# An attention block with a mixture of experts: the first part ordered anew, places' experts found on partitions, and own memory for each third first matrix

## The chip, the cores and the metric

The kernel runs on one core of a Trainium2 chip. The metric is the device time of one execution in microseconds (us); it is given as the median of three runs. The engines are TensorE (PE; its weight loads are listed as PEld), VectorE (DVE), ScalarE (ACT), GpSimd (POOL) and SyncE (SP), which here only issues transfers. Each engine works through its own list in order and waits on semaphores of the others.

## The reference

The input x has 2 sequences of 2048 tokens with 256 channels. It is normalized once, and the result goes into two branches whose outputs are added to x.

```python
xn = layernorm(x)
# branch 1: time mixing
h = layernorm(xn) * ln_g + ln_b
last = shift h by one token (zero at the start of a sequence)
k = (h * mix_k + last * (1 - mix_k)) @ Wk.T      # v and r alike
num, den = scans over the tokens: num = num * td + exp(k) * v ; den = den * td + exp(k)
a = sigmoid(r) * (num / (den + 1e-8)) @ Wo.T
# branch 2: a mixture of 8 experts, 2 for each token
s = relu(xn @ Wr + br); the best two of 8, softmax over them
f = sum over the two of weight * (relu(xn @ W1[e] + b1[e]) @ W2[e] + b2[e])
out = x + a + f
```

## The kernel before, in words

The 4096 tokens are cut into 8 blocks of 512 tokens, four per sequence; a block is held as four rows of 128 tokens on the partitions. The kernel has two parts.

The first part does, for each block: `stats` (mean and variance of its four rows with bn_stats and bn_aggr on VectorE, L190 and L191, then a power of -0.5 on POOL, L200), `normed` (both normalizations at once: x2 = (x - mean) * rr for each row, three rows on VectorE, L224, and one on ScalarE, L226; then a write of x2 to a table in HBM), `turned` (eight transposes on TensorE, L244, copied by ScalarE into x2T for the router and, with ln_g and ln_b, into xaT for the time mixing, L247 and L248; xaT has one more column in front, the last token of the block before, which POOL writes, L237 or L239), `scored` (router products, L262), and `routed` (the scores turned back, L273).

Then there are the mixes. Each block needs three blends of now and last (k, v, r), numbered 0k, 0v, 0r, 1k and so on to 7r. `mix(n)` makes the next n of the 24 blends: for blocks 0 to 2 VectorE forms dx = now - last (L301) and then two operations L310 for each blend; for blocks 3 to 7 ScalarE first makes last * (1 - mix) (L285, two steps for each blend, which `pieces` issues one after each of its own steps once NFIRST steps are done), and VectorE adds the rest (L310). `some(n)` makes the next n of the 48 pieces: one output half of a projection, two matrix products on TensorE (L339, four records in the profile) and one ScalarE eviction into kvr (L342). Blend i serves pieces 2i and 2i + 1.

When all eight blocks are routed, `best_two` on VectorE finds each token's two experts (L371 to L394); two products with a triangle and with ones (`pre`, L559) give each token's rank; a long list of small VectorE operations (L572 to L655) turns ranks into places. A loop of eight groups over `inv` (L736 to L755) then builds one-hot tables on VectorE and multiplies them on TensorE, which gives the token of each place: `into` and `frm`. `experts_of_places` finds which expert each place belongs to (`whose`, `whose_i`): a place is a pair of units of 128 tokens or a single unit, and the expert is the number of limits that lie at or below the place's number. It does so with all 39 places along the free axis, the same in each partition. `experts_later` fills `mine` (L722), a mask by place and expert.

The second part is a loop over 37 steps, one for each place. Each gathers its tokens' rows from the table (POOL, L874), loads one expert's matrices (`load_first`: b1 and w1, L857 and L859; `load_second`: b2 and w2, L865 and L867; all issued on SP, with the expert's number read from whose_i), and does two products (hp at L914, yp at L927). The scans, gates and output products of the time mixing are spread over its first steps.

The order is fixed by hand: under `tc.manual_schedule()` each engine executes in the order in which the program text issues. The calls of stats, normed, mix, some and so on from L408 to L1003 are therefore the schedule, and `keep_warm(n)` puts n matrix products without use (L405) into TensorE's list. Memory is taken from pools; a pool opened after another is closed can lie on the memory of the closed one, and its first writers then wait for the last users of that. wpool, with the experts' matrices, is opened after the routing pool is closed and waits in this way. A pool's `bufs` gives how many buffers of one tag rotate: w1 and b1 have three, mixes six, x2 three, the tables of the inv loop three.

Of the kernel before, what the change touches and what calls it, by code (L numbers as in the profile page):

```python
# [9 lines left out]
F32 = mybir.dt.float32  # L10
# [4 lines left out]
ALU = mybir.AluOpType  # L15
# [11 lines left out]
def rwkv_moe_block(  # L27
# [47 lines left out]
    KMAX = (NU + 1) // 2  # L75
# [14 lines left out]
    small = ctx.enter_context(tc.tile_pool(name="small", bufs=2))  # L90
    kvr_pool = ctx.enter_context(tc.tile_pool(name="kvr", bufs=NB // 2))
# [67 lines left out]
    nc.vector.memset(power, -0.5)  # L159
    prio = rout.tile([P, NT, E], F32, name="prio")  # L160
# [24 lines left out]
    def stats(b, i0=0, i1=NS):  # L185
        if i0 == 0:
            mvs[b] = (mk(f"st_{b}", [P, NS, 6]), mk(f"mv_{b}", [P, NS, 2]))
        st, mv = mvs[b]
        for i in range(i0, i1):
            nc.vector.bn_stats(st[:, i, :], xts[b][:, i, :])  # L190
            nc.vector.bn_aggr(mv[:, i, :], st[:, i, :])  # L191
        if i1 < NS:
            return
        mean, var = mv[:, :, 0], mv[:, :, 1]

        at = ts(b, NS)
        w = mk(f"w_{b}", [P, NS])
        nc.gpsimd.tensor_scalar(w, var, 1.0 + LN_EPS, LN_EPS * LN_EPS, ALU.mult, ALU.add)
        rrs[b] = rr_all[:, at]
        nc.gpsimd.tensor_tensor(rrs[b], w, power[:, 0:NS], ALU.pow)  # L200
        nc.gpsimd.tensor_scalar(ve_all[:, at], var, LN_EPS, 0.0, ALU.add, ALU.add)
        mrrs[b] = (mean, mk(f"mrr_{b}", [P, NS]))
# [12 lines left out]

    def normed(b):
        xt = xts[b]
        mean, mrr = mrrs[b]
        nc.vector.scalar_tensor_tensor(mrr, mean, -1.0, rrs[b], ALU.mult, ALU.mult)
        x2 = x2s[b] = rpool.tile([P, NS, C], F32, tag="x2", bufs=3, name=f"x2_{b}")  # L220
        for t in range(NS):
            r, m = rrs[b][:, t : t + 1], mrr[:, t : t + 1]
            if t:
                nc.vector.tensor_scalar(x2[:, t, :], xt[:, t, :], r, m, ALU.mult, ALU.add)  # L224
            else:
                nc.scalar.activation(x2[:, t, :], xt[:, t, :], AF.Identity, bias=m, scale=r)  # L226
        nc.sync.dma_start(table_t[:, ts(b, NS), 0:C], x2)

    x2Ts = [None] * NB

    def turned(b):
        x2 = x2s[b]
        x2T = x2Ts[b] = rpool.tile([P, NC, TB], F32, tag="x2T", name=f"x2T_{b}")

        xaT = xaTs[b] = xa_pool.tile([P, NC, TB + 1], F32, name=f"xaT_{b}")
        if b % BPS == 0:
            nc.gpsimd.memset(xaT[:, :, 0:1], 0.0)  # L237
        else:
            nc.gpsimd.tensor_copy(xaT[:, :, 0:1], xaTs[b - 1][:, :, TB : TB + 1])  # L239
        tps = []  # L240
        for c in range(NC):
            tp = ps_t.tile([P, TB], F32, tag="pt", name=f"tp_{b}_{c}")
            for t in range(NS):
                nc.tensor.transpose(tp[:, ts(t, P)], x2[:, t, ts(c, P)], ident)  # L244
            tps.append(tp)
            if b:
                nc.scalar.copy(x2T[:, c, :], tp)  # L247
            nc.scalar.activation(  # L248
                xaT[:, c, 1 : TB + 1], tp, AF.Identity, bias=vec(5, c), scale=vec(4, c)
            )  # L250
        if b == 0:
            for c in range(NC):
                nc.scalar.copy(x2T[:, c, :], tps[c])
# [40 lines left out]
    def blender():  # L294
        for b in range(NB):
            now, last = xaTs[b][:, :, 1 : TB + 1], xaTs[b][:, :, 0:TB]
            if b < NDX:

                dx = mixes.tile([P, NC, TB], F32, tag="dx", bufs=1, name=f"dx_{b}")
                for c in (slice(0, 1), slice(1, NC)) if b == 0 else (slice(0, NC),):  # L300
                    nc.vector.tensor_tensor(dx[:, c, :], now[:, c, :], last[:, c, :], ALU.subtract)  # L301
            for i in range(3):
                if b < NDX:
                    m = mixes.tile([P, NC, TB], F32, tag="mix", name=f"mix{i}_{b}")
                    by, other = dx, last
                else:
                    m = ahead.pop(0)
                    by, other = now, m
                for c in range(NC):
                    nc.vector.scalar_tensor_tensor(  # L310
                        m[:, c, :], by[:, c, :], vec(1 + i, c), other[:, c, :],
                        ALU.mult, ALU.add,
                    )
                blends[b].append(m)
                yield
# [9 lines left out]
    NFIRST = 12  # L325
# [80 lines left out]

    keep_warm(13)
# [51 lines left out]
    k_iota = count("k_iota", KMAX)  # L459
    u_iota = count("u_iota", NSING, base=2 * NPAIR)  # L460
# [23 lines left out]
    keep_warm(8)  # L484
    some(2)
    turned(1)
    nc.scalar.activation(td, cols[:, E * NH : E * NH + NC], AF.Exp)
    mix(2)
    some(2)
    scored(0)  # L490
    stats(2)
    stats(3)
    normed(2)
# [4 lines left out]
    mix(1)  # L498
    some(1)
    routed(1)  # L500
    normed(3)
    mix(1)
    some(1)
    turned(3)
    scored(2)
    some(1)
    stats(4)
    mix(1)
# [3 lines left out]
    turned(4)  # L512
    scored(3)
    stats(5)
    stats(6)
    divisors(0)
# [3 lines left out]
    turned(5)  # L520
    some(1)
    scored(4)
    stats(7)
    normed(6)
    some(1)
    routed(4)
    turned(6)
    scored(5)
    normed(7)
    divisors(1)  # L530
    mix(1)
    some(1)
    routed(5)
    turned(7)
    scored(6)
# [4 lines left out]
    mix(1)  # L540
# [27 lines left out]
    mix(3)  # L568
# [56 lines left out]
    mix(1)  # L625
    some(2)
    pos = rt("pos", (P, E, NT))
# [30 lines left out]
    some(2)  # L658
# [6 lines left out]
    def holds(nm, places, limits):  # L665

        n, k = places.shape[1], limits.shape[1]
        c = rt(f"{nm}_c", (P, n, k))
        nc.vector.tensor_tensor(
            c, places.unsqueeze(2).to_broadcast([P, n, k]),  # L670
            limits.unsqueeze(1).to_broadcast([P, n, k]), ALU.is_ge,
        )
        r = rt(f"{nm}_r", (P, n))
        nc.vector.tensor_reduce(r, c, AX.X, ALU.add)
        return r

    whose = rt("whose", (P, NW))

    def experts_of_places():
        limits = rt("limits", (P, 3, E))  # L680
        nc.vector.tensor_copy(limits[:, 0, :], fcum[:, 0, :])
        nc.vector.tensor_scalar(limits[:, 1, :], fcum[:, 1, :], full, None, ALU.add)
        nc.vector.tensor_scalar(limits[:, 2, :], fcum[:, 2, :], pairs, None, ALU.add)
        by_pair = holds("by_pair", k_iota, limits.rearrange("p a e -> p (a e)"))
        nth = rt("nth", (P, NSING))
        taken = rt("taken", (P, 1))
        nc.vector.tensor_scalar(taken, pairs, float(NPAIR), pairs, ALU.max, ALU.add)
        nc.vector.tensor_scalar(nth, u_iota, taken, None, ALU.subtract)
        by_single = holds("by_single", nth, fcum[:, 2, :])

        for i, n in enumerate((full, pairs)):
            after = rt(f"after{i}", (P, KMAX))
            nc.vector.tensor_scalar(after, k_iota, n, float(-E), ALU.is_ge, ALU.mult)
            nc.vector.tensor_tensor(by_pair, by_pair, after, ALU.add)
        nc.vector.tensor_copy(whose[:, 0:NPAIR], by_pair[:, 0:NPAIR])

        split = rt("split", (P, NSING))
        nc.vector.tensor_scalar(split, nth, 0.0, None, ALU.is_lt)
        n = KMAX - NPAIR
        part = rt("part", (P, 2 * n))  # L700
        nc.vector.tensor_copy(
            part.rearrange("p (a b) -> p a b", b=2),
            by_pair[:, NPAIR:KMAX].unsqueeze(2).to_broadcast([P, n, 2]),
        )
        part = part[:, 0:NSING]
        nc.vector.tensor_tensor(part, part, by_single, ALU.subtract)
        nc.vector.tensor_tensor(part, part, split, ALU.mult)
        nc.vector.tensor_tensor(whose[:, NPAIR:NW], part, by_single, ALU.add)
        nc.vector.tensor_scalar_min(whose, whose, float(E - 1))
        nc.vector.tensor_copy(whose_i, whose)  # L710
# [19 lines left out]
    MIX, SOME = (0, 1, 0, 1, 0, 1, 0, 1), (1, 1, 1, 2, 1, 1, 1, 0)  # L730
# [37 lines left out]
    nc.vector.tensor_scalar_min(frm, into, float(NTOK - 1))  # L768
    experts_of_places()
    mix(2)  # L770
    some(2)
# [82 lines left out]
    def load_first(s):  # L854
        ev = expert_of(s)
        b1_sb = wpool.tile([P, NH], F32, tag="b1", bufs=3, name=f"b1_{s}")
        nc.sync.dma_start(b1_sb, b1cols[bass.ds(ev, 1)].rearrange("a p h -> p (a h)"))  # L857
        w1_sb = wpool.tile([P, NC, H], F32, tag="w1", bufs=3, name=f"w1_{s}")
        nc.sync.dma_start(w1_sb, w1[bass.ds(ev, 1)].rearrange("a (c p) h -> p (a c) h", p=P))  # L859
        weights[s, 1] = (w1_sb, b1_sb)  # L860
# [89 lines left out]
    some(4)  # L950
# [115 lines left out]
```

## Time and profile before

| what | value |
|---|---|
| median of three runs | 665.88 us (664.79 to 666.34) |
| the profiled execution's own time | 665.95 us |
| its span | 664.3 us |
| mean granted TensorE clock | 0.99 |
| TensorE busy | 638.8 us, 96% |
| VectorE busy | 338.0 us, 51% |
| ScalarE busy | 230.4 us, 35% |
| POOL busy | 233.1 us, 35% |
| first hp product | 126.12 us from the start of the span |
| VectorE busy from 57.30 to 101.25 | 41.17 us of 43.95 |

How to read it: the span is the time from the first to the last recorded instruction, and the execution's own time has 1.65 us around it. Busy times are averages over the whole span, so an engine with a low share can still hold up another in one stage; that is read from the timeline and from the waits. An entry `a <- b` reads "a is made from b", and a bracket at the end of a row gives the idle time of the engine ahead of it and who ended it. The clock is the share of full speed that TensorE was granted.

### The profile page before, as it was taken

Reading aid. Unit: us, or ns where it says so; the run is one execution under the profiler, and the core shown is the slowest. Engines: PE = TensorE matmul, PEld = TensorE weight load, DVE = VectorE, ACT = ScalarE, POOL = GpSimd, SP = SyncE. Lnnn points to the kernel's source line nnn. Section 1 sums busy time; section 2 is a strip of 40 time slices with the busy share of each in tenths; the row PEclk is TensorE's granted clock in tenths of the full one; section 3 lists DMA queues with packets and bytes.
Section 4 is the critical chain, followed back from the end, with each engine's and each line's share of the span. In section 5 each row is a group of like instructions: output and inputs, shape, how many; then the busy total and the mean of one; then the engine's idle time right before and its main releaser. Section 6 shows DMA issues by size and latency. Waiting matters only on the chain. (4 is left out here: it accounts for less than half of the span.)

```text
span 664.3 us, 9082 instructions
## 1 busy us (share of the span) xinstructions
PE 638.8 (96%) x3038; PEld 498.2 (75%) x3038; DVE 338.0 (51%) x777; ACT 230.4 (35%) x474; POOL 233.1 (35%) x207
## 2 busy tenths in 40 slices
PE   7989997999999999999999999999999999999993
PEld 3544443688888888888888888888888888888882
DVE  7987996456356458576666667422222121222110
ACT  3776753423423323333333333222223222223320
POOL 5460204033343335313443434643434433334111
PEclk9999997999999999999999999999999999999998
DMA  8529101767976986699868686976566777666621
GB/s 279 167 96 299 19 1 50 238 210 215 308 186 196 298 202 196 178 341 254 225 166 227 170 223 142 269 185 205 168 176 182 215 213 220 168 176 182 200 34 17
DMA packets 92409, 124.50 MB, mean 187 GB/s; under 512 B 15452, under 2 KB 80552, under 8 KB 92232
## 3 DMA queue, kind: packets, MB, share of 16 engines
q1 hardware_dynamic: 74368, 100.99, 46.7%
q0 software_dynamic: 17472, 22.86, 18.6%
q8 instruction: 25, 0.41, 0.2%
q14 instruction: 24, 0.20, 0.1%
q10 hardware_dynamic: 520, 0.05, 0.1%
HBM read 105.89 MB, written 26.38 MB: 199 GB/s over the span
## 5 line engine op out<-in xcount | busy, mean ns | idle before, releaser
L918 ACT ACTIVATE h<-hp,b 128x256 f32<-128x256 f32 (+1 forms) x296 | 135.8, 459 | 348.5 <-PE hp L914 237.5
L914 PE MATMUL hp<-xT,w 128*128 128x256 f32 (+1 forms) x1184 | 251.8, 369 | 1.1 <-ACT h L918 0.4
L927 PE MATMUL yp<-w,h 128*128 128x256 f32 x1104 | 244.4, 379 | 0.0
L914 PEld LDWEIGHTS hp<-xT,w 128*128 128x128 f32 x1184 | 198.8, 189 | 49.5 <-ACT h L918 16.1
L927 PEld LDWEIGHTS yp<-w,h 128*128 128x128 f32 x1104 | 207.0, 190 | 26.6
L939 POOL DMA_INDIRECT out_dram<-y,into x50 | 82.4, 1648 | 213.5 <-DVE y L935 98.6
L904 DVE COPY xT<-xp 128x512 f32<-128x512 f32 (+1 forms) x37 | 24.3, 655 | 168.5 <-PE xp L902 163.3
L874 POOL DMA_INDIRECT xg<-table,frm x69 | 75.2, 1090 | 45.1 <-PE p L339 24.3
L934 DVE TENSOR_TENSOR y<-yp,b 128x256 f32<-128x256 f32 x67 | 28.3, 423 | 105.1 <-PE yp L927 105.1
L939 POOL DMA_INDIRECT acc<-y,into x19 | 31.9, 1679 | 92.9 <-issue 34.7
L813 DVE RECIPROCAL dn<-dn 128x512 f32<-128x512 f32 x16 | 53.6, 3353 | 0.5
L342 ACT ACTIVATE kvr<-p 128x512 f32<-128x512 f32 x48 | 28.7, 599 | 41.4 <-PE p L339 40.8
L339 PE MATMUL p<-mix,wr 128*128 128x512 f32 x64 | 32.7, 650 | 4.5 <-DVE mix L310 4.1
L339 PE MATMUL p<-mix,wk 128*128 128x512 f32 x64 | 30.1, 603 | 3.9 <-DVE mix L310 2.4
L339 PE MATMUL p<-mix,wv 128*128 128x512 f32 x64 | 29.6, 599 | 0.0
L822 PE MATMUL op<-wo,z 128*128 128x256 f32 x128 | 28.9, 379 | 0.0
L339 PEld LDWEIGHTS p<-mix,wr 128*128 128x128 f32 x64 | 12.7, 207 | 19.5 <-issue 17.0
L822 PEld LDWEIGHTS op<-wo,z 128*128 128x128 f32 x128 | 24.3, 190 | 3.3
L935 DVE TENSOR_SCALAR y<-y,gate 128x256 f32<-128x256 f32 x67 | 24.6, 367 | 2.4
L310 DVE SCALAR_TENSOR_TENSOR mix<-xaT,cols,mix 128x512 f32<-128x512 f32 x30 | 22.0, 779 | 7.0 <-ACT mix L285 6.9
L339 PEld LDWEIGHTS p<-mix,wk 128*128 128x128 f32 x64 | 11.5, 190 | 16.6 <-issue 12.2
L884 DVE TENSOR_SCALAR xg<-xg 128x256 f32<-128x256 f32 x69 | 22.1, 359 | 0.0
(176 smaller groups left out, 402.6 us busy)
## 6 DMA issues: line engine op xcount, KB each, us to landing
w<-in_L_ffn_W_dram SPq DMA_DIRECT2D x74, 1024.0 KB
b<-in_L_ffn_b_dram SPq DMA_DIRECT2D x37, 128.0 KB
table<-x SPq DMA_DIRECT2D x8, 512.0 KB
x<-in_L_attn_x_dram SPq DMA_DIRECT2D x7, 512.0 KB
out_dram<-o_sb POOLq DMA_DIRECT2D x5, 512.0 KB
acc<-o_sb POOLq DMA_DIRECT2D x3, 512.0 KB
xg<-table,frm POOLq DMA_INDIRECT x69
out_dram<-y,into POOLq DMA_INDIRECT x50
```

The source lines that it names most:

```text
L339: nc.tensor.matmul(p, w[:, c, ts(o, P)], m[:, c, :], start=(c == 0), stop=(c == NC - 1))
L342: nc.scalar.activation(kvr[b][:, i, o, :], p, f, scale=sign)
L813: nc.vector.reciprocal(dn, dn)
L822: nc.tensor.matmul(op, z[:, c, ts(t, P)], wo_sb[:, c, :], start=(c == 0), stop=(c == NC - 1))
L874: nc.gpsimd.indirect_dma_start(out=g, out_offset=None, in_=table, in_offset=bass.IndirectOffsetOnAxis(ap=frm[:, u : u + 1], axis=0), bound ...
L904: nc.vector.tensor_copy(xT, xp)
L914: nc.tensor.matmul(hp, w1_sb[:, c, ts(j, P)], xT[:, c, :], start=(c == 0), stop=(c == NC - 1))
L918: nc.scalar.activation(h[:, 0:n], hp, AF.Relu, bias=b1_sb[:, j : j + 1])
L927: nc.tensor.matmul(yp, hs[j][:, ts(i, P)], w2_sb[:, j, :], start=(j == 0), stop=(j == NH - 1))
L934: nc.vector.tensor_tensor(y, yp, b2_sb, ALU.add)
L935: nc.vector.tensor_scalar(y, y, gates[s][i], None, ALU.mult)
L939: return nc.gpsimd.indirect_dma_start(out=to, out_offset=bass.IndirectOffsetOnAxis(ap=into[:, u : u + 1], axis=0), in_=y, in_offset=None, ...
```

## The change

The diff does these things.

1. `stats`: the four bn_stats of a block are issued in a row and then the four bn_aggr, instead of in turns. The factor mrr = -mean * rr is made on POOL by two operations instead of one on VectorE.
2. `normed`: VectorE makes all four rows of blocks 0, 4, 5, 6 and 7 and three rows of blocks 1, 2 and 3; it takes mean and rr as they are, (x - mean) * rr. ScalarE makes the first row of blocks 1, 2 and 3.
3. The first column of xaT is written by `follow(b)`, which is called at other places than `turned(b)`; that of block 0 is cleared before the first statistics.
4. The order of the first part is written anew: divisors(0) comes after the statistics of block 3; 12 pieces stand ahead of the last `routed` instead of 15; nine blends stand ahead of best_two instead of ten; four blends follow it; in the inv loop the blends and pieces are (1, 1, 0, 1, 0, 1, 1, 1) and (1, 1, 1, 2, 1, 1, 1, 1). A blend and two pieces come between `frm` and `experts_of_places`. NFIRST is 10 instead of 12, and a blend whose ScalarE step has not been issued issues it itself. `keep_warm(8)` becomes `keep_warm(11)`.
5. `experts_of_places` has the places on the partitions, one per partition: each comparison is one small operation with a per-partition scalar, the counts are one reduction, and the resulting expert per partition is spread over all partitions by putting it on a diagonal (`on_row`) and multiplying by ones on TensorE, into a PSUM tile `whose`. Constant tiles for this (place, at_pair, wlim, offs, held) are made at the start.
6. The first matrices of steps 0, 3, 6, ... are held in a pool of their own, w1_own, which is opened at the start with one buffer; wpool keeps two buffers for the others.
7. dx moves to another pool (rpool), and pos uses the memory of cand.

```diff
     def stats(b, i0=0, i1=NS):
...
         for i in range(i0, i1):
             nc.vector.bn_stats(st[:, i, :], xts[b][:, i, :])
+        for i in range(i0, i1):
             nc.vector.bn_aggr(mv[:, i, :], st[:, i, :])
...
+        nc.gpsimd.tensor_scalar(less_mean, mean, -1.0, 0.0, ALU.mult, ALU.add)
+        nc.gpsimd.tensor_tensor(mrr, less_mean, rrs[b], ALU.mult)
         nc.gpsimd.tensor_scalar(ve_all[:, at], var, LN_EPS, 0.0, ALU.add, ALU.add)
...
+    NORMED = (0, 4, 5, 6, 7)
     def normed(b):
-        nc.vector.scalar_tensor_tensor(mrr, mean, -1.0, rrs[b], ALU.mult, ALU.mult)
...
-            if t:
-                nc.vector.tensor_scalar(x2[:, t, :], xt[:, t, :], r, m, ALU.mult, ALU.add)
+            if t or b in NORMED:
+                nc.vector.tensor_scalar(
+                    x2[:, t, :], xt[:, t, :], mean[:, t : t + 1], r, ALU.subtract, ALU.mult
+                )
...
+    def follow(b):
+        if b > 0 and b % BPS:
+            nc.gpsimd.tensor_copy(xaTs[b][:, :, 0:1], xaTs[b - 1][:, :, TB : TB + 1])
+        elif b > 0:
+            nc.gpsimd.memset(xaTs[b][:, :, 0:1], 0.0)
...
+                    while not ahead:
+                        next(preparing)
                     m = ahead.pop(0)
...
-    NFIRST = 12
+    NFIRST = 10
...
     normed(1)
-    keep_warm(8)
+    keep_warm(11)
     some(2)
     turned(1)
+    follow(1)
...
     scored(4)
+    stats(6)
+    mix(1)
     some(1)
     normed(6)
     routed(4)
     turned(6)
+    follow(5)
     scored(5)
+    stats(7)
+    mix(1)
+    some(1)
     normed(7)
     routed(5)
     turned(7)
...
-    mix(3)
+    mix(4)
     some(4)
...
-    whose = rt("whose", (P, NW))
+    whose = ps_t.tile([P, NW], F32, tag="pt", name="whose")
     def experts_of_places():
-        by_pair = holds("by_pair", k_iota, limits.rearrange("p a e -> p (a e)"))
...
+        nc.vector.scalar_tensor_tensor(
+            held[:, 0, :], lim.rearrange("p a e -> p (a e)"), at_pair, wlim,
+            ALU.is_le, ALU.mult,
+        )
...
+        nc.vector.tensor_scalar(held[:, 1, 0:E], fcum[:, 2, :], nth, None, ALU.is_le)
+        nc.vector.tensor_reduce(by, held, AX.X, ALU.add)
...
+        nc.vector.tensor_scalar(on_row, ident[:, 0:NW], expert, None, ALU.mult)
+        nc.tensor.matmul(whose, ones, on_row, start=True, stop=True)
         nc.vector.tensor_copy(whose_i, whose)
...
-    MIX, SOME = (0, 1, 0, 1, 0, 1, 0, 1), (1, 1, 1, 2, 1, 1, 1, 0)
+    MIX, SOME = (1, 1, 0, 1, 0, 1, 1, 1), (1, 1, 1, 2, 1, 1, 1, 1)
...
     nc.vector.tensor_scalar_min(frm, into, float(NTOK - 1))
+    mix(1)
+    some(2)
     experts_of_places()
-    mix(2)
-    some(2)
+    some(1)
     mix(1)
     some(2)
     mix(1)
...
     def load_first(s):
-        b1_sb = wpool.tile([P, NH], F32, tag="b1", bufs=3, name=f"b1_{s}")
+        pool = wpool if s % 3 else w1_own
+        b1_sb = pool.tile([P, NH], F32, tag="b1", name=f"b1_{s}")
...
-        w1_sb = wpool.tile([P, NC, H], F32, tag="w1", bufs=3, name=f"w1_{s}")
+        w1_sb = pool.tile([P, NC, H], F32, tag="w1", name=f"w1_{s}")
```

The reductions over `by` then give the expert: where the place lies ahead of the single units its pair's count, otherwise the count of the singles, held to 7 at most. The values that the kernel computes are the same.

## The prediction

> **What bounds the kernel now.** I read the page first, then the busy time by stage, then the list of TensorE's waits, then the timeline around each wait.
>
> The page, its span and its clock row (tenths of full speed, 40 slices of 16.6 us):
>
> ```profile
> span 664.3 us, 9082 instructions
> ...
> PEclk9999997999999999999999999999999999999998
> ```
>
> One slice in mid-kernel, near 100 to 116 us, has a low TensorE clock. Busy time by stage (start:end, length, then PE, PEld, DVE, ACT, POOL, and the clock):
>
> ```profile
> 14.00:57.30 43.30, 39.71 (x253) 20.64 (x253) 35.97 (x100) 31.18 (x61) 21.20 (x37) 1.00 0.55 183
> 57.30:101.25 43.95, 42.76 (x159) 19.67 (x159) 41.17 (x97) 28.01 (x48) 4.79 (x7) 1.00 0.23 60
> 101.25:126.12 24.87, 20.80 (x44) 8.93 (x44) 14.94 (x49) 8.76 (x15) 7.35 (x6) 0.86 0.32 95
> 126.12:654.00 527.88, 526.51 (x2551) 445.10 (x2549) 236.62 (x492) 158.09 (x345) 192.07 (x139) 1.00 0.72 204
> ```
>
> The experts' loop (last row) begins with the first hp product at 126.12. TensorE is idle there for 1.4 us of 528, at full clock: it is the bound, and the change adds nothing to it. So the question is only when hp can begin. Before it, TensorE idles for 3.6, 1.2 and 4.1 us in three stages, and VectorE is nearly as busy as TensorE in the second. The waits of TensorE (total, times, longest):
>
> ```profile
> PE p L339 <- DVE mix L310: 6.5, 2, 4.1
> ...
> PE p L339 <- ACT xaT L248: 1.5, 1, 1.5
> PE inv L755 <- DVE oh_t L747: 1.2, 1, 1.2
> ```
>
> The 4.1 is the largest. Its place in the timeline (start, us, engine, line, operation):
>
> ```profile
> 101.28 0.23 DVE L761 SCALAR_TENSOR_TENSOR empty<-inv,less 128x71 f32<-128x71 f32 x1 [1.40 <-PE inv L755]
> ...
> 107.83 0.18 DVE L710 CAST whose_i<-whose 128x39 int32<-128x39 f32 x1
> 107.93 4.06 DVE L310 SCALAR_TENSOR_TENSOR mix<-xaT,cols,mix 128x512 f32<-128x512 f32 x6
> ...
> 108.82 6.73 PE L339 MATMUL p<-mix,wr 128*128 128x512 f32 x8 [4.07 <-DVE mix L310]
> ...
> 115.38 3.60 PE L339 MATMUL p<-mix,wk 128*128 128x512 f32 x8
> ```
>
> VectorE works out the experts of the places from 102.33 to 108.01 and only then makes the blend that TensorE needs. The same eight matmul records take 6.73 us there and 3.60 just after: microsecond by microsecond the granted clock is 0.50 from 109 to 115. The stall costs 4.07 + (6.73 - 3.60) = 7.2 us.
>
> **The change, part by part.** A "piece" is one projection output: four records, 1.72 us (two pieces start 3.44 apart, 69.36 to 72.80). I follow TensorE to hp.
>
> *Start.* xaT's first column is now cleared early. Before, dx waited 1.73 us for that memset (POOL, 11.50); now ScalarE's xaT ends it. normed(0) has its four rows on VectorE: 7.71 to 9.1 instead of 8.77, and xaT comes 0.3 later, so dx starts near 10.3 instead of 11.63 and the first blend ends at 13.1 instead of 14.35. The three more warm matmuls (0.24 each) end near 12.3, before the first piece at 12.5; were they late they would cost at most that difference, 0.7. Four more memsets (0.07 each) and two at_pair operations (about 0.15 each) lie ahead of waits for x or pow: nothing, or at most 0.5.
>
> *Statistics in a row.* Before, one aggregate follows each bn_stats:
>
> ```profile
> 29.05 0.42 DVE L190 BATCH_NORM_STATS2 st<-x 128x6 f32<-128x256 f32 x1
> ...
> 29.50 0.18 DVE L191 BATCH_NORM_AGGREGATE mv<-st 128x2 f32<-128x6 f32 x1
> ...
> 29.60 0.39 DVE L190 BATCH_NORM_STATS2 st<-x 128x6 f32<-128x256 f32 x1
> ```
>
> The dependent aggregate starts only after bn_stats has ended (0.45 after its start), while the independent bn_stats starts 0.10 after the aggregate, before that one's 0.18 is over. So a block costs 4 x 0.53 = 2.13 now; in a row 4 x 0.35 (three independent x rows take 1.06, L224) + 4 x 0.10 = 1.8, saving 0.33. The Trainium skill speaks against it: "VectorE: DVE Perf Modes", Terms, says that a flush follows every operation and the next can't issue until the pipe is empty. Then a block costs 4 x (0.39 + 0.18) = 2.3 in either order, and nothing is saved. The 0.10 row contradicts that for independent work, so I take 1.8.
>
> *Rows of x.* mrr leaves VectorE (7 x about 0.2 with its wait) for POOL (less_mean and mrr, each 0.2 to 0.5 by L198 and L563; 0.25 taken). Blocks 0, 4 to 7 have a fourth row on VectorE: 0.35 each. This takes away the 1.37 us wait of tp for ScalarE's row at 39.78, but ScalarE still has the rows of blocks 1 to 3.
>
> *Block stage, VectorE from the first blend (13.1) to normed(7).* Six statistics 10.8, 25 rows x 0.353 = 8.8, blends 0v 0r 1k 1v 1r 2k of 1.41 = 8.5, two dx of 1.22: 30.5. Add 0.45 for rows slowed by POOL's iotas (1.51 instead of 1.06 at 14.46). The same sum for the kernel before is 30.3 plus its two waits for pow (0.92 and 1.54), 32.8, against 32.4 in the timeline. After, at least 1.4 us of other work lies between a block's statistics and its rows; pow takes 0.2 + 1.05. rs (2.97 us) now stands on POOL ahead of block 4's pow and should end near 26.5, block 4's statistics at 27.3. I allow 0.8 for waits: normed(7) ends at 44.9 (46.77 before). The copies of xaT's column are later on POOL but still ahead of their blends. Table writes issue on SP in the old order; their three x2 buffers are needed again some 9 us after the write, so nothing.
>
> TensorE then has turned(7) 1.05, two scored 1.15, two pieces 3.6, two routed 0.2 and 0.1 of latency: routed(7) at 51.0 instead of 57.28. But 12 pieces lie before it instead of 15; three, 5.2 us, go behind it. **Gain 1.1.**
>
> *Middle.* Five pieces (8.6) to pre at 59.6; best_two took 57.06 to 64.76, so hot is ready near 58.7. Blend 4k needs ScalarE's first step earlier than pieces bring it; the forced one is done near 60.5, used at 62.8. Then VectorE: four blends 5.65, cum to delta 5.0 (68.50 to 73.52), pos 1.8, a blend 1.9 (2.25 under POOL's work before), posk to lohi 2.9, a blend 1.4, first tables 1.45: 78.7. TensorE reaches inv after 13 pieces, 82.2. The wait of 1.19 at 84.45 goes: **gain 1.2.** In the inv loop five blends instead of three lie before the last tables: 78.7 + 7 x 1.45 + 5 x 1.42 = 96.0, and TensorE comes to them at 98.5. Cover 2.5 us; without it each microsecond is one.
>
> *Tail.* With inv done at T, three pieces (5.2) follow and then the new whose matmul. VectorE: empty to frm 1.15 (101.28 to 102.42), a blend 1.41, eleven small operations of 0.10 (independent) to 0.27 (dependent): 1.1 to 3.0, taken 2.2; 4.8 to 4.9 in all. Behind whose stand p6r1 and p7k, whose blends exist. The matmul costs 0.05 to 0.3 by the inv (0.05) and pre (0.27) rows; 0.15 taken. whose_i is ready at T + 5.5, 7v at T + 7, wanted at T + 10.6. So the stall is gone: **gain 7.2**, less up to 1.1 if the small operations are all slow.
>
> *Memory of the first matrices.* Three buffers in the same rotation as before. w1_0 no longer waits for "mine" (118.77, issue 118.98): it can go near 105, hp comes near 116.6. Before, issue to hp was 7 us and no wait showed, so hidden. w2_0 still waits for "mine", near 108, and is wanted near 120. Nothing.
>
> Sum: 1.1 + 1.2 + 7.2 = **9.5 us**. hp moves from 126.12 to 116.6, the span from 664.3 to 654.8. The profiled execution took 665.95 with 1.65 around its span, 0.07 from the median of 665.88 (664.79 to 666.34). So **656.4 us**. A measurement can tell 0.2%, 1.3 us, from no change.
>
> **The rivals.**
>
> *One half-clock period.* Before tp7, TensorE ends its work near 42.6 and normed(7) comes at 44.9: 2.4 us idle. In this trace the clock stayed 1.00 through idle times of 1.50 (48.84) and 2.42 (13.74), and fell after 4.07. The Trainium skill ("TensorE: Matmul & The Clock Gate", Part 1) puts the threshold at one idle window of 3.4 us, which spares us. But its Part 4 says that transposes don't count as busy in the same way; from 42.6 to the next projection at 46.6 that is 4.0 us. By that rule the clock halves, and the sum is worse by the 3.1 that it cost at 109: **659.5**. The row: 45.62 to 48.84 held only transposes, small products and idling, 3.2 us, at 1.00. I stay with the row, narrowly.
>
> *Statistics save nothing.* Six blocks x 0.33: routed(7) 2.0 later: **658.4**.
>
> *VectorE is late in the inv loop or for whose.* Against it stand 2.5 and 0.3 us of cover. Two microseconds late gives **658.4**; a full return of the old stall, 7.2, gives 663.6.
>
> *The reordering does nothing but remove the tail's stall*, the block stage giving nothing back: 658.7.
>
> *Slower.* The block stage stays at half clock. TensorE has 3.5 us of work per block there, against VectorE's 4.6; at half clock 7.0. If the waits before tp4 to tp7 each hold the clock down, TensorE sets the pace, loses 2.4 x 4 and then 3.1 until dense work restores it, some 12.7 against 9.5: **669**. It decides from 19 us at half clock on. Against it: each wait before tp7 is below 1.4.
>
> **How the numbers follow.** As worked out 0.58 (own range 654.5 to 658); one half-clock period 0.13; statistics or block stage give nothing 0.13; VectorE late 0.10; slower 0.05; no measurable change 0.01. Range 653.8 to 660.8: it holds the first three and most of the fourth. Faster 0.93, same 0.02, slower 0.05.
>
> **What would show it.** routed(7) near 51; no wait of 1 us at the first inv; whose on TensorE without a wait over 0.5; the clock at 1.00 from 100 to 120; the first hp near 116.6; the rest still 538 us. Wrong would be: a wait over 3.4 us before tp7 with clock 0.50 after it, aggregates in a row 0.2 apart, or TensorE waiting for oh_t or on_row.

## The result and the profile after

The changed kernel takes 656.75 us (median of 4 runs, 654.95 to 657.24) beside 665.56 us (664.79 to 666.34) for the kernel before on the same chip: a ratio of 0.9863, 95% interval 0.984 to 0.9885. The profiled execution took 656.74 us, its span is 655.0, so 1.74 us lie around it.

The page of the changed kernel, its span and its clock row (tenths of full speed, 40 slices of 16.4 us):

```profile
span 655.0 us, 9090 instructions
...
PEclk9999999999999999999999999999999999999997
```

The low slice in mid-kernel is gone. The busy time by stage, cut at the same events as before (the first blend, the last routing, the last inv, the first hp product), but here at the start of the last routing and of the last inv, which end at 51.87 and 99.53; the cuts before, 57.30 and 101.25, lie at their ends (start:end, length, then PE, PEld, DVE, ACT, POOL, the clock, DMA share, GB/s):

```profile
14.00:51.60 37.60, 35.17 (x240) 18.25 (x238) 33.40 (x95) 26.43 (x51) 28.09 (x49) 1.00 0.56 184
51.60:99.10 47.50, 47.50 (x165) 21.79 (x164) 43.80 (x100) 32.10 (x54) 4.80 (x7) 1.00 0.27 78
99.10:117.17 18.07, 18.07 (x54) 8.36 (x53) 10.77 (x38) 7.19 (x12) 6.74 (x6) 1.00 0.61 180
117.17:646.00 528.83, 526.43 (x2551) 445.07 (x2549) 236.26 (x492) 158.50 (x345) 192.22 (x140) 1.00 0.71 202
```

From 51.60 on TensorE has no idle time until hp, and the clock is full. The stages hold other numbers of pieces than before (three pieces have moved behind routed(7)), so their lengths can't be set against each other row by row; the idle time can: 3.6, 1.2 and 4.1 us before, 2.4, 0 and 0 now. The loop behind hp did not change: 537.8 us from hp to the end of the span, against 538.2. Nearly the whole gain is hp at 117.17 instead of 126.12: 8.95 of the 9.3 us by which the span is shorter. All waits of TensorE that are left (total, times, longest):

```profile
PE warm L437 <- DVE restart L190: 2.3, 1, 2.3
PE colp L446 <- DMA wr_sb<-in_L_ffn_Wr_dram: 1.6, 1, 1.6
PE tp L274 <- DVE x L246: 1.5, 1, 1.5
PE tp L274 <- ACT x L250: 0.8, 1, 0.8
PE p L371 <- DVE mix L342: 0.2, 1, 0.2
```

The last row is where 6.5 us stood, 2.42 of them at the first piece and 4.07 in the tail. The timeline of the tail (start, us, engine, line, operation; a bracket is idle time ahead), the answer to the stall at 107.93 before:

```profile
100.62 1.41 DVE L342 SCALAR_TENSOR_TENSOR mix<-xaT,cols,mix 128x512 f32<-128x512 f32 x2
101.95 0.15 DVE L704 COPY offs<-fcum 128x1 f32<-128x1 f32 x1
...
104.06 0.49 DVE L731 TENSOR_SCALAR on_row<-ident,expert 128x39 bf16<-128x39 f32 x1
104.84 0.20 DVE L733 CAST whose_i<-whose 128x39 int32<-128x39 f32 x1 [0.28 <-PE whose L732]
104.95 2.73 DVE L342 SCALAR_TENSOR_TENSOR mix<-xaT,cols,mix 128x512 f32<-128x512 f32 x4
```

and TensorE's rows in the same stretch:

```profile
102.89 1.88 PE L371 MATMUL p<-mix,wr 128*128 128x512 f32 x4
104.61 0.18 PE L732 MATMUL whose<-on_row,ones 128*128 128x39 bf16 x1
104.63 1.96 PE L371 MATMUL p<-mix,wr 128*128 128x512 f32 x4
106.43 3.60 PE L371 MATMUL p<-mix,wk 128*128 128x512 f32 x8
109.86 3.60 PE L371 MATMUL p<-mix,wv 128*128 128x512 f32 x8
```

The experts of the places take VectorE from 101.95 to 104.55, and the blend that p7v needs at 109.86 is the first half of the last row shown for VectorE, done near 106.3 (the second half, to 107.7, is the blend for p7r). The groups of eight records take 3.60 us, none 6.73.

### The profile page after: what moved, and what is told of

Same layout as the page of the kernel before. It is cut to its first block, busy times and chain, and to the rows that moved or that the text cites. A ratio compares the mean times of both kernels' runs of the same rounds, so it can differ in the third digit from the quotient of the medians.

```text
span 655.0 us, 9090 instructions
## 1 busy us (share of the span) xinstructions
PE 637.1 (97%) x3042; PEld 497.9 (76%) x3042; DVE 333.5 (51%) x771; ACT 228.6 (35%) x469; POOL 238.9 (36%) x222
## 5 line engine op out<-in xcount | busy, mean ns | idle before, releaser
L371 PE MATMUL p<-mix,wr 128*128 128x512 f32 x64 | 29.9, 600 | 0.1
L371 PEld LDWEIGHTS p<-mix,wv 128*128 128x128 f32 x64 | 11.7, 190 | 12.8 <-issue 11.4
L315 ACT ACTIVATE mix<-xaT,unmixed 128x512 f32<-128x512 f32 x30 | 21.4, 712 | 0.0
```

The source lines that it names most:

```text
L371: nc.tensor.matmul(p, w[:, c, ts(o, P)], m[:, c, :], start=(c == 0), stop=(c == NC - 1))
```

## The experiments

My theory: the tail's 7.2 us come from the order of VectorE's list, the rest from the statistics in a row and the earlier start. The rivals to be told apart from it: the shorter search does it; the own memory of the first matrices does it; the fourth row on VectorE does it; the clock takes part of the gain back ahead of block 7.

"hp" is the start of the first hp product in the profiled execution, and "before" the median of the kernel before, measured beside it. Executions of the same code differ by up to 1.9 us in when they come to block 7 (the end of `sp` at 43.42 in the changed kernel and at 41.55 in e7), so where two traces are compared there, I take the time from the end of `sp` ahead of block 7's transposes (43.42 us after the change) to hp: 73.75 us in the changed kernel.

### e1: the old kernel with two blends ahead of the search

```diff
-    experts_of_places()
     mix(2)
+    experts_of_places()
     some(2)
```

> The kernel before, with one edit: the two blends 6r and 7k are made ahead of the search for the places' experts instead of behind it. My theory (it is the order of VectorE's list that stalls TensorE, not the length of the search): with inv done at T, frm is ready at T+1.2, 6r and 7k at T+4.0, whose_i at T+9.6, 7v at T+11.0, where TensorE wants it at T+10.3. A wait of 0.7 us instead of 4.07, clock 1.00, 6.5 us gained: 659.4 us, 660 if w1_0, which waits for mine (T+13.3), lands late. Rival (the search itself has to be short): TensorE still waits over 2 us and less than 4 us are gained, 662 or more.

Measured: 661.93 us (661.47 to 663.17, 5 runs; before 665.33), ratio 0.9956 (0.9939 to 0.9972). The stall is gone with this one line moved. TensorE's rows in the tail of e1:

```profile
108.92 3.60 PE L339 MATMUL p<-mix,wk 128*128 128x512 f32 x8
112.66 3.67 PE L339 MATMUL p<-mix,wv 128*128 128x512 f32 x8
...
116.61 3.60 PE L339 MATMUL p<-mix,wr 128*128 128x512 f32 x8
121.73 2.49 PE L914 MATMUL hp<-xT,w 128*128 128x256 f32 x10 [1.53 <-DMA w<-in_L_ffn_W_dram]
```

From the last inv's end to hp it takes 19.6 us, against 24.9 before and 17.6 after. So the order is worth 5.3 us of the tail's 7.2 here. Most of the rest turned into a new wait, which I had called hidden: with the blends ahead of it, the search ends later (`mine` 115.23), the first matrix, which shares its memory with what is released there, is issued at 116.47, and hp stands 1.53 us for it. The median gains 3.4 us and not 5.3. The profiled execution came to the end of the last inv 0.9 us later (102.13 against 101.24), with one stretch of half clock at 14.6 to 18.0 us on the way; that lies ahead of the edit and has nothing to do with it. The time alone would not have decided, since the rival had named a gain of less than 4 us; what decides is that TensorE's wait for a blend in the tail, 4.07 us before, is gone.

### e2, e3, e4: the changed kernel with the old search, with shared memory, with both

e2 puts the old `experts_of_places` back into the new order:

```diff
-    whose = ps_t.tile([P, NW], F32, tag="pt", name="whose")
+    whose = rt("whose", (P, NW))
...
     def experts_of_places():
...
+        by_pair = holds("by_pair", k_iota, limits.rearrange("p a e -> p (a e)"))
...
-        nc.vector.tensor_scalar(on_row, ident[:, 0:NW], expert, None, ALU.mult)
-        nc.tensor.matmul(whose, ones, on_row, start=True, stop=True)
```

e3 takes w1_own away; e4 does both:

```diff
-    w1_own = ctx.enter_context(tc.tile_pool(name="w1_own", bufs=1))
...
-        pool = wpool if s % 3 else w1_own
...
-        w1_sb = pool.tile([P, NC, H], F32, tag="w1", name=f"w1_{s}")
+        w1_sb = wpool.tile([P, NC, H], F32, tag="w1", bufs=3, name=f"w1_{s}")
```

> The changed kernel with the old search for the places' experts (all places along the free axis, 5.6 us of VectorE instead of 2.2, no product with ones). My theory: the new order has room for it. whose_i at T+8.2, 7v at T+9.6, wanted at T+10.4; no wait of TensorE, first hp at 117.1, 656.7 us, no difference that can be measured. Rival (the search on partitions is what gains): TensorE waits again, 3 to 7 us, 660 to 664 us.

> The changed kernel with all first matrices in one pool of three buffers, as before. w1_0 then waits for mine (108.9) and is issued about 3.3 us later, near 110; it lands within some 5 us, 115, and is wanted at 117.2. My theory: hidden, 656.7 us. Rival (own memory gains): hp waits 1 to 3 us for the matrix, 658 to 660 us.

> Both undone at once: old search and shared memory of the first matrices, in the new order. whose_i at T+8.2, 7v and 7r until T+11, mine at T+12.3 (111.8), w1_0 issued near 112.8, landing near 117.8 where TensorE is ready for it at 117.1. My theory: each part alone is hidden, but together the cover is used up: hp waits 0 to 1.5 us, 656.8 to 658.2 us. Rival (parts independent): 656.7 us and no wait.

| | median (runs) | ratio (interval) | hp | hp waits for w1_0 |
|---|---|---|---|---|
| changed kernel | 656.75 (4) | 0.9863 (0.984 to 0.9885) | 117.17 | 0 |
| e2 old search | 655.51 (4) | 0.9851 (0.9833 to 0.9869) | 117.60 | 0 |
| e3 shared w1 | 658.14 (4) | 0.9885 (0.9862 to 0.9909) | 118.31 | 0.30 |
| e4 both | 657.43 (4) | 0.9886 (0.9863 to 0.9909) | 116.47 | 0.82 |

e2 is as fast as the changed kernel within what can be told. VectorE in e2's tail:

```profile
102.49 0.16 DVE L719 COPY limits<-fcum 128x8 f32<-128x8 f32 x1
...
102.96 1.06 DVE L707 TENSOR_TENSOR by_pair_c<-k_iota,limits 128x864 f32<-128x864 f32 x1
104.05 1.05 DVE L712 TENSOR_REDUCE by_pair_r<-by_pair_c 128x36 f32<-128x864 f32 x1
...
107.97 0.18 DVE L748 CAST whose_i<-whose 128x39 int32<-128x39 f32 x1
108.06 2.73 DVE L343 SCALAR_TENSOR_TENSOR mix<-xaT,cols,mix 128x512 f32<-128x512 f32 x4
```

The old search takes 5.7 us (102.49 to 108.15) where the new one takes 3.1 with its matmul (101.95 to 105.04), and TensorE still finds its blends: the blend behind it starts at 108.06 and is wanted at 110.30. So the shorter search is not what removes the stall. It leaves more cover, and it makes `mine` earlier (108.41 against 111.52), which is worth something only without the own memory: e4's wait of 0.82 against e3's 0.30. The rows of the first hp product in e3 and in e4:

```profile
118.31 7.24 PE L937 MATMUL hp<-xT,w 128*128 128x256 f32 x32 [0.30 <-DMA w<-in_L_ffn_W_dram]
116.47 7.24 PE L952 MATMUL hp<-xT,w 128*128 128x256 f32 x32 [0.82 <-DMA w<-in_L_ffn_W_dram]
```

The own memory is thus worth 0.3 us with the new search and 0.8 with the old one; I had expected e3's wait to be hidden. The medians of e3 and e4 lie 1.4 and 0.7 us above the changed kernel's, but the intervals overlap, and e3's profiled execution has two other losses (half clock at 45.8 to 49.2, and 0.7 us for the first wk); only the hp wait is the memory's.

### e5: the statistics in turns again

```diff
             nc.vector.bn_stats(st[:, i, :], xts[b][:, i, :])
-        for i in range(i0, i1):
             nc.vector.bn_aggr(mv[:, i, :], st[:, i, :])
```

> The changed kernel with bn_stats and bn_aggr in turns again. In a row a block took 1.59 us (27.02 to 28.61), in turns 2.13: 0.53 more for each of six blocks ahead of normed(7), 3.2 us. My theory: TensorE waits for normed(7), so the delay reaches it one for one and is kept to the end: routed(7) near 54.8 instead of 51.6, hp near 120.3, 659.8 us. Rival (a flush after every operation): nothing, 656.7. Rival (the waits for pow take the delay up): up to 1.7 less, 658.2.

Measured: 658.05 us (656.7 to 659.57, 4 runs; before 665.11), ratio 0.9881 (0.9859 to 0.9904), 1.3 us above the changed kernel's median, intervals overlapping; the trace says more. One block's statistics in the changed kernel (four bn_stats as one row, then four aggregates, then the next block's):

```profile
27.02 1.40 DVE L208 BATCH_NORM_STATS2 st<-x 128x6 f32<-128x256 f32 x4
28.33 0.36 DVE L210 BATCH_NORM_AGGREGATE mv<-st 128x2 f32<-128x6 f32 x4
28.61 1.37 DVE L208 BATCH_NORM_STATS2 st<-x 128x6 f32<-128x256 f32 x4
```

That is 28.61 - 27.02 = 1.59 us for a block; in e5 it is 28.87 - 26.73 = 2.14, from the rows:

```profile
26.73 0.42 DVE L208 BATCH_NORM_STATS2 st<-x 128x6 f32<-128x256 f32 x1
27.19 0.18 DVE L209 BATCH_NORM_AGGREGATE mv<-st 128x2 f32<-128x6 f32 x1
...
28.87 0.40 DVE L208 BATCH_NORM_STATS2 st<-x 128x6 f32<-128x256 f32 x1
```

In e5 the waits of TensorE for rows of x are 2.8 us in three instead of 1.5 in one (2.07 ahead of block 7), and routed(7) comes at 54.32 instead of 51.60. Of these 2.7 us about 1.4 are a stretch of half clock at 46.9 to 50.3, which the changed kernel's profiled execution doesn't have, and 1.3 are the delay.

So my theory of 3.2 us, one for one, failed. From the end of the first blend to the end of normed(7) e5 takes 32.7 us, the changed kernel 31.6. Six blocks at 0.55 more are 3.3, but two things take most of it back: POOL's tables for the inv loop also come later (15.25 instead of 14.27), so that the rows of block 1, at 14.26, are done as they begin, in 1.16 us instead of 2.73; and the 0.52 us wait for pow ahead of block 4's rows is gone. The second rival, which had the waits for pow in mind, comes nearest in time.

### e6: the first row of blocks 4 to 7 on ScalarE again

```diff
-    NORMED = (0, 4, 5, 6, 7)
+    NORMED = (0,)
```

> The changed kernel with the first row of blocks 4 to 7 on ScalarE again (mrr made on POOL). VectorE has four rows less, 1.3 us. If VectorE alone paces the block stage, routed(7) comes up to 1.3 us earlier, 655.5 us. If the row waits behind other work on ScalarE, as for block 5 in the kernel before (1.37 us) and block 3 in the changed one (0.79), TensorE waits for it instead: 657 to 658.5 us. I expect the second, 657.3.

Measured: 656.16 us (656.07 to 656.66, 4 runs; before 665.11), ratio 0.9862 (0.9842 to 0.9882): the same time. TensorE's waits in the block stage change hands:

```profile
PE tp L274 <- ACT x L250: 3.2, 5, 1.0
```

The five waits for ScalarE (longest 1.0) come to 3.2 us, against 0.8 + 1.5 in two. routed(7) comes at 50.60 instead of 51.60, but this execution's first piece had started 1.3 us earlier (12.24 against 13.54): from the first piece to routed(7) it takes 38.4 us against 38.1. The waits went where I had expected them, and cost nothing that can be told, where I had expected 0.6 us. The fourth row on VectorE brings nothing: it trades several short waits for a long one ahead of block 7.

### e7, e8: a longer wait ahead of block 7

Two and four additions of 128x512 into a spare tile stand ahead of normed(7) on VectorE; nothing reads the tile, so what the kernel computes is the same.

```diff
     some(1)
+    for _ in range(2):
+        nc.vector.tensor_tensor(spare[:, 1, :], spare[:, 0, :], spare[:, 0, :], ALU.add)
     normed(7)
```

> The changed kernel with two additions of 128x512 without use on VectorE ahead of normed(7) (about 0.67 us each). TensorE's wait before tp7 grows from 1.53 to 2.8 us, and the time without projections there from 3.7 to 5.0. If the clock goes by whole idle time and the bound lies between 2.4 and 4.07, it stays 1.00 and the cost is the delay, 1.3 us: 658.0. If transposes and small products don't count, the clock falls to 0.50 near 46 and about 3 us more are lost: 661.

> The same with four additions: a wait of 4.2 us. As in the kernel before after 4.07 us, the clock falls to 0.50 for about 6 us: delay 2.7 and 3.1 more, 662.5 us. If the clock stays at 1.00: 659.4.

Measured, one run each: 657.18 us with a wait of 2.51 ahead of block 7, 660.07 us with a wait of 4.01. From `sp` to hp the changed kernel takes 73.75 us, e7 2.3 more, e8 4.95 more. Of e7's 2.3, 0.98 is the longer wait and 1.3 the clock (block 7's transposes to the end of routed(7): 8.22 us against 6.91); of e8's 4.95, 2.48 and 2.47. The times alone would have misled: e7's lies below the 658.0 that was expected for a full clock, because this execution came to block 7 1.9 us earlier, and yet its clock was halved. The clock in e8, microsecond by microsecond (columns as in the table by stage):

```profile
44.00:45.00 1.00, 0.00 (x0) 0.00 (x0) 0.97 (x2) 0.00 (x0) 1.00 (x2) 1.00 0.00 0
45.00:46.00 1.00, 0.33 (x2) 0.28 (x2) 1.00 (x4) 0.00 (x0) 1.00 (x2) 0.50 0.00 0
...
50.00:51.00 1.00, 1.00 (x3) 0.48 (x2) 0.09 (x1) 0.00 (x0) 0.00 (x0) 0.50 1.70 524
51.00:52.00 1.00, 1.00 (x2) 0.02 (x1) 0.00 (x0) 0.00 (x0) 0.00 (x0) 0.59 0.00 0
```

So half a clock ahead of block 7 is a real danger; its price there is 1.3 to 1.6 us for one stretch of 3.4 us (block 7's transposes to routed(7) in e2, e3, e5 and e7 against the changed kernel) and 2.5 for the two in e8.

### e9, e10, e11: what was still waiting

The traces named a loss that no part of the change touches: block 1's rows, which take 1.02 to 1.06 us for three elsewhere, take 2.73 us while POOL writes its index tables. VectorE and then POOL in the changed kernel:

```profile
14.06 2.73 DVE L246 TENSOR_SCALAR x<-x,mv,rr_all 128x256 f32<-128x256 f32 x3
```

```profile
14.27 1.52 POOL L485 IOTA lo_iota<- 128x256 f16 x1
15.76 0.88 POOL L485 IOTA hi_iota<- 128x142 f16 x1
```

e9 makes these tables ahead of the first statistics, where POOL waits for the input anyway. The moved code is `count`, its calls and the rest of that block, unchanged:

```diff
+    def count(nm, n, dtype=F32, base=0, step=1, chan=0, pool=rout):
...
+    e_iota = count("e_iota", E)
...
     keep_warm(13)
     stats(0)
```

> The changed kernel with most of POOL's constants (upper, lo_iota, hi_iota, e_iota, token, rest_row) made ahead of the first statistics, where POOL idles for 4.9 us. In the changed kernel three rows of block 1 took 2.73 us on VectorE (14.06) while POOL made them, against 1.05 elsewhere. My theory: the two engines slow each other; the rows take 1.05, VectorE is 1.7 us ahead, waits for pow take part of it, and 0.5 to 1.5 us of TensorE's wait of 1.53 before tp7 go: 655.6 us. Rival (the rows wait for something else): they stay at 2.7, 656.7 us.

Measured: 654.42 us (653.98 to 654.95, 5 runs; before 665.33), ratio 0.983 (0.9815 to 0.9846): 2.3 us below the changed kernel in the median, though the two intervals just touch. VectorE's row at the same place:

```profile
13.55 1.16 DVE L246 TENSOR_SCALAR x<-x,mv,rr_all 128x256 f32<-128x256 f32 x3
```

2.73 became 1.16, and from the first blend to normed(7) it takes 30.09 us instead of 31.66: just these 1.57. The wait ahead of block 7 falls from 1.53 to 0.68. hp comes 2.09 us earlier; 0.52 of that is this execution's earlier start, and 1.57 are left.

e10 has, on top of e9, the statistics of blocks 6 and 7 one block ahead, so that POOL's powers are ready when the rows want them. It also puts block 3's first row on VectorE, `divisors(0)` behind the last statistics, and a blend behind normed(7), so it can't say which of these does what:

```diff
-    NORMED = (0, 4, 5, 6, 7)
+    NORMED = (0, 3, 4, 5, 6, 7)
...
-    divisors(0)
     normed(2)
...
     normed(5)
+    stats(6)
     some(1)
...
-    stats(6)
+    stats(7)
+    normed(6)
     mix(1)
     some(1)
-    normed(6)
...
-    stats(7)
-    mix(1)
+    divisors(0)
     some(1)
     normed(7)
...
-    mix(2)
+    mix(3)
```

> As e9, and besides the statistics of blocks 6 and 7 one block earlier (ahead of the rows of blocks 5 and 6 or just behind), so that pow is always covered, rs of the first half after the last pow, dx and blend 2k behind normed(7), and block 3's first row on VectorE. VectorE then has normed(7) ready about 4 us earlier. TensorE's idle times of 0.79 and 1.53 in the block stage go, 2.3 us, and no more, since TensorE then sets the pace: first hp near 114.9, 654.4 us. Rival: the new order makes other waits (ScalarE's copies or POOL), 655.5 to 657.

Measured: 654.26 us (652.97 to 654.48, 5 runs; before 665.33), ratio 0.9823 (0.9806 to 0.9839). No wait for rows of x is left, and routed(7) comes at 47.47, 2.0 us earlier than e9's 49.51; but hp comes only 0.56 earlier. The waits of TensorE show where it went:

```profile
PE pre L594 <- DVE hot L426: 1.3, 1, 1.3
```

VectorE had stood 2.53 us for the second `rs`, a power of 16 columns on POOL; the first, at 41.33, had taken 4.23 us there, and the new order had pushed both back:

```profile
46.22 3.42 POOL L228 TENSOR_TENSOR rs<-ve_all,power 128x16 f32<-128x16 f32 x1
49.67 0.19 DVE L233 TENSOR_TENSOR sd<-rs,inv_rr 128x32 f32<-128x32 f32 x1 [2.53 <-POOL rs L228]
```

e11 is e10 with the first of the two moved into a stretch in which POOL is idle:

```diff
     stats(5)
+    divisors(0)
     normed(4)
...
     scored(5)
-    divisors(0)
     some(1)
```

> The version with the statistics a block ahead left one new wait: pre stood 1.3 us for hot, because VectorE came to undivided() at 46.80 and waited 2.53 us for POOL's second rs (46.22, 3.42 us), which was queued behind the first rs (41.33, 4.23 us). Here the first rs moves into POOL's idle stretch near 33 us, behind the statistics of block 5. If that queue is the cause, hot is ready some 2 to 3 us earlier, pre doesn't wait, and the kernel takes 652.9 to 653.3 us, with the first hp near 113.2. If POOL's rs delays the pow of block 6 by more than its idle 2 us, a wait of tp for normed(6) of 0.5 to 1 us comes back and the time stays at 654.2.

Measured: 652.89 us (652.05 to 653.41, 5 runs; before 665.41), ratio 0.9806 (0.9792 to 0.9819). All waits of TensorE in e11:

```profile
PE warm L437 <- DVE restart L190: 2.3, 1, 2.3
PE colp L483 <- DMA wr_sb<-in_L_ffn_Wr_dram: 0.8, 1, 0.8
PE p L371 <- DVE mix L342: 0.2, 1, 0.2
```

`hot` is ready at 55.6 instead of 57.6, `pre` doesn't wait, hp starts at 113.47. From the first piece to hp TensorE waits for nothing in this list: what is left ahead of hp is its own work and the start. This version beats both kernels.

## Why the prediction was right, and where it wasn't

| step | predicted | measured |
|---|---|---|
| first blend ends | 13.1 | 14.15 |
| statistics of a block in a row | 1.8 | 1.59 |
| waits of VectorE for pow | 0.8 | 1.71 |
| normed(7) ends | 44.9 | 45.78 |
| TensorE's wait ahead of block 7 | 2.4 | 1.53 |
| routed(7) ends | 51.0 | 51.87 |
| routed(7) to the first inv | 31.2 | 30.96 |
| last tables done, TensorE comes to them | 96.0, 98.5 | 95.8, 99.1 |
| the search, without its matmul | 2.2 | 2.6 |
| first inv to hp | 34.4 | 34.34 |
| hp | 116.6 | 117.17 |
| hp to the end | 538.2 | 537.8 |

*The sum.* 9.5 us were expected and the span is 9.3 shorter. The middle gave 1.4 (1.2 predicted) and the tail 7.3 (7.2), each by the mechanism that was named: the wait at the first inv and the stall at p7v are both gone. Up to routed(7), with the three pieces that moved behind it set aside, only 0.3 came of 1.1. This is where hp's error of 0.6 comes from: 0.9 are lost up to routed(7), and the middle gives 0.2 back. That the order removes the stall is shown (e1); that it is the moved pieces and blends which remove the wait at the first inv is read from the rows, and no run tests it alone.

*Start.* "The first blend ends at 13.1" was 1.05 early: `colp` waited 1.59 us for a transfer in this execution (0.5 to 0.8 in e9, e10 and e11). The prediction followed only the memset that had held dx before, not what came next. But in e2, e3, e4, e6, e7 and e8, where colp doesn't wait, the first blend ends at 12.7 to 13.5, with 13.1 in the middle: the loss belongs to this execution more than to the change.

*Block stage.* The term that was wrong is "0.45 for rows slowed by POOL's iotas": the slowing cost 2.73 - 1.05 = 1.7 (1.3 in e2, e4, e6, e7 and e8, where the rows took 2.33), because the rows now lie wholly beside the iotas. Waits for pow were 0.9 more than allowed. Two terms in the other direction hid most of this: the statistics took 0.21 less per block (six blocks: 1.3), and rows of x 0.325 each in place of 0.353 (25: 0.7). From the first blend to normed(7) predicted and measured differ by 0.2 only because these cancel, which is luck; what is missing at routed(7) is the late start.

*Statistics in a row.* The rule of the Trainium skill that the next operation can't issue before the pipe is empty ("VectorE: DVE Perf Modes", Terms) would have given 2.3; 1.59 against e5's 2.14 decides for the row. TensorE gets less of it: in e5 it was delayed by 1.3 us, not by six times 0.55. Four bn_stats follow one another at 0.325 us and independent aggregates at 0.07, less than the 0.10 assumed.

*Memory of the first matrices: "nothing".* Right against the old order, wrong in the new one: in e1, e3 and e4 hp waits 1.53, 0.30 and 0.82 us for w1_0. With the stall gone its cover is gone as well, so the new memory protects the gain.

*The search.* The prediction put the tail's gain on order and search together. e1 and e2 split it: the order alone removes the stall. The new search in the old order was not run; by its rows it is 2.6 us shorter, so it would have left some 1.5 of the 4.07 us (an estimate).

*Rows of x.* "This takes away the 1.37 us wait of tp for ScalarE's row" is right as to the wait, but a 1.53 us wait for VectorE stands in its place (e6).

*Rivals.* "One half-clock period" was given a price of 3.1 us and a place ahead of block 7. The place is right: with the same wait of 1.53 the clock stayed full in the changed kernel's profiled execution and was halved in e2's and e3's. The price was taken from two periods in a row; one costs 1.3 to 1.6. The row that I stayed with, 3.2 us without projections at full clock, had not settled it. The reading by which only an idle window of 3.4 us counts does not fit e2 and e3, where TensorE was idle for 1.53 us. The reading by which transposes don't count as busy fits better but isn't shown: in e2 the halving sets in 2.7 us after the last projection, before 3.4 us without one are over. It is a scatter around the predicted outcome: of the changed kernel's four runs, those at 656.76 and 657.24 have a mean clock of 0.992, as e2's and e3's profiled executions with one period have, those at 654.95 and 656.74 of 0.996 and 0.995. So this rival probably happened in two of the four runs, and that the median lies within 0.4 us of 656.4 is in part luck. "Statistics save nothing" is refuted by e5's rows. "The reordering does nothing but remove the tail's stall" was near the truth up to routed(7) (0.3 us), not in the middle (1.4). "VectorE late" did not come about: the cover in the inv loop was 3.3 us, and TensorE waited nowhere for `on_row`. "Slower" needed 19 us at half clock, and there were none in the profiled execution and 3.4 in e2's and e3's.

## What to carry to other kernels

When an engine makes both short, urgent inputs and a long result that is wanted later, first put the urgent ones ahead in its list; making the long work shorter is a second step, and here it was not needed. When a stall goes, look at once for what it had covered: here a matrix load that would have arrived 0.3 to 1.5 us late, and in e10 a power on POOL whose delay had been harmless. Look also for work on one engine that slows another beside it, since no list of waits names it; only a row that takes 2.6 times its usual duration does.

## What the runs showed of the hardware

*The clock was halved in whole periods, and the same short wait started one or did not.* Summed over the microsecond rows, the half-clock time is 3.4 us in e1, e2, e3, e5 and e7, 6.84 in the kernel before (108.15 to 114.99), 6.82 in e8: one or two times 3.4. Block 7's first transposes in the changed kernel, where the clock stayed full, and in e2, where it did not:

```profile
44.96 1.65 PE L274 MATMUL tp<-ident,x 128*128 128x128 f32 x8 [1.53 <-DVE x L246]
43.90 2.13 PE L275 MATMUL tp<-ident,x 128*128 128x128 f32 x8 [1.53 <-DVE x L247]
```

The clock in e2 (columns as above):

```profile
44.00:45.00 1.00, 1.00 (x5) 0.51 (x6) 1.00 (x4) 0.00 (x0) 1.00 (x3) 0.95 0.07 16
45.00:46.00 1.00, 1.00 (x9) 0.67 (x9) 1.00 (x3) 0.73 (x2) 1.00 (x1) 0.50 0.30 109
...
48.00:49.00 1.00, 1.00 (x3) 0.52 (x2) 0.29 (x1) 0.00 (x0) 0.00 (x0) 0.84 2.77 865
49.00:50.00 1.00, 1.00 (x18) 0.38 (x16) 0.00 (x0) 0.35 (x1) 0.00 (x0) 1.00 0.50 197
```

Ahead of block 7 the halving sets in 2.7 to 3.5 us after the end of the last projection, in e2, e3, e5 and e7 when TensorE is already at work on block 7's transposes, in e8 while it still waits; a wait of 1.53 us is enough (e2, e3), and the same wait left the clock at 1.00 in the changed kernel's profiled execution, although 3.8 us lay between its projections. In the same way the 2.42 us wait ahead of the first piece left the clock full in the kernel before and is followed by a halving in e1. The Trainium skill ("TensorE: Matmul & The Clock Gate", Part 1) gives a free-running window of 3413 ns. The length agrees; that the window's phase decides between the two outcomes would explain them, but it is argued here and not shown, and what counts as busy within a window stays open. Kernels without a long wait there (e6, e9, e10, e11) spread by 0.6 to 1.5 us over their runs, the others with several runs by 1.7 to 2.9.

*POOL's work slows VectorE's rows.* Three rows of 128x256 took 2.73 us beside POOL's iotas and 1.16 without them, both where the iotas were moved (e9) and where they began only as the rows ended (e5). In the other direction there is only a coincidence in the rows: in the changed kernel POOL's `less_mean` of 128x4 takes 0.18 to 0.19 us for five blocks and 0.51 to 0.63 for three, and these three lie beside VectorE's `dx` or a blend (0.59 at 11.61, beside `dx`).
